# A twelve-layer macaron kernel: the first maxima of the 16-head attentions are computed in the layers before them

## The chip, the cores and the metric

The kernel runs on one core of a Trainium2 chip, as one program. The metric is the device time of one execution in microseconds (us); "before" is the median of three runs. One execution was also profiled, and every view shown comes from it. PE is TensorE (PEld its weight loads), DVE VectorE, ACT ScalarE, POOL GpSimd, SP the queue that issues most DMAs.

## The reference

The input x has 2048 tokens of 128 channels (attentions see it as batches of one sequence; the kernel treats it as 2048 rows). Twelve layers follow each other, each adding to x what it computes from the layer-normed x:

```python
x = x + 0.5 * ffn0(ln(x)); x = x + attn0(ln(x)); x = x + 0.5 * ffn0(ln(x))
x = x + 0.5 * ffn1(ln(x)); x = x + attn1(ln(x)); x = x + 0.5 * ffn1(ln(x))
x = x + 0.5 * ffn2(ln(x)); x = x + attn2(ln(x)); x = x + 0.5 * ffn2(ln(x))
x = x + 0.5 * ffn3(ln(x)); x = x + attn3(ln(x)); x = x + 0.5 * ffn3(ln(x))
```

Four of them matter here.

- `ffn1` is a mixture: a router (a second layer norm, eight logits, softmax, the best two), and for each token a shared and eight routed experts `silu(x Wg) * (x Wu) Wd`, all of them computed for all tokens and weighted with the router's gates.
- `attn1` has 16 heads of 8 channels and no mask: `softmax(q k^T / sqrt(8)) v`, then a projection and a bias.
- `ffn2` quantises the normed x in blocks of 32 channels to a six-bit grid and multiplies by one quantised 128 x 128 weight.
- `attn2` is like `attn1`, with rotary embedding on q and k and no bias.

## The kernel before, in words

The 2048 tokens are four chunks of 512 (`NC` = 4, `CH` = 512), each of four blocks of 128 (`TC` = 4). x stays on the chip as `xs[0..3]`. `STAGES` lists the twelve layers; each is a `Stage` whose body is a Python generator. A stage yields an estimate in us after each small piece of its front; `io.lead(passed)` in the running stage takes that much off the next stage's due time, and lets it emit its next piece once it is due. So a stage's front is written out beside the work of the stage before. `yield True` ends the front, and the stage then runs when its turn comes. `io.ready(c)` says whether the previous stage has finished chunk c, `io.mark(c)` reports it. A compiler turns the written order into a static order per engine; it may move instructions by its own estimates, but not those given to `tc.keep_in_program_order`, which keep their order among each other. `tc.high_priority()` lets instructions go ahead of earlier ones.

**The mixture** (`ffn1`). For each chunk c and each of nine experts: `up` makes twelve products of 128 x 512 (L227 to L229: values are kept as a high and a low part, three products each) into `pg` and `pu`, ACT takes SiLU (`sg`, L715), DVE multiplies (`h`, L717). One expert later `down` makes `pd` (L725), which DVE adds to x with the gate (L735). After the fifth expert the next chunk's own front (norm, transpose, router) is emitted at once. In chunks 2 and 3, `io.lead(4.3)` follows each expert.

**The 16-head attention** (`packed` and `flash`). Heads are taken four at a time; four groups by four query chunks are 16 iterations. Keys of one group and chunk are stacked by DMA into a tile `km`, queries into `qt` (`stack_k`, `stack_q`, L1379), with each head on 32 rows (high, low, high parts beside each other). Stream A is the first pass: a step is two score matmuls of 32 rows by 128 x 512 (L1069) into one of two double PSUM banks and one DVE maximum over both (`mp`, L1087). An iteration has 4 row blocks x 4 key chunks x 2 head pairs = 32 steps. Then `put_max` writes the maxima, and `put` makes the queries of the second pass (`q2`, L1561). Stream B is the second pass: scores once more (L1190), the exponential on ACT (`pt`, L1199), the products with v (`pv`, L1136). `flash` interleaves A and B by columns: all of iteration 0 of A runs first, then `leads` and a skew say how far A stays ahead of B. All matmuls of A and B keep their program order on PE (`pe`).

What `packed` emits ahead of its turn are norms, transposes and keys of chunks 0 to 2 and the queries of chunk 0. The tiles `km` and `qt`, their memsets on POOL (L1494, L1496), the stacking and all steps come after `yield True`. The hook of the first step makes chunk 3's keys.

**The small layer** (`ffn2`, k = 0). Its chunks 0 to 2 are emitted beside the mixture; at chunk 3 it calls `io.lead(9.0)` nine times, which emits fronts of `attn2` there. `quantised` is some eleven DVE and POOL instructions over 128 x 512 (L776 to L793).

PSUM has three single banks (tag `s2`), two double ones (`s1`) and one for `pv`.

Of the kernel before, what the change touches and what calls it, by code (L numbers as in the profile page):

```python
# [64 lines left out]
def tile_macaron(ctx: ExitStack, tc: tile.TileContext, a: dict, out: bass.AP, stages=STAGES):  # L65
# [159 lines left out]
    def product(ps, w, x, start=True, stop=True):  # L225
        (wh, wl), (xh, xl) = w, x
        nc.tensor.matmul(ps, wh, xh, start=start, stop=False)  # L227
        nc.tensor.matmul(ps, wh, xl, start=False, stop=False)  # L228
        nc.tensor.matmul(ps, wl, xh, start=False, stop=stop)  # L229
# [434 lines left out]
    def ffn1(io, k, w, early):  # L664
# [3 lines left out]
        def front(c, pool):  # L668
            n = 1 if pool is early and k else 2
            xf = layer_norm(c)  # L670
            xT = high_low(turned(xf), pool, "xT", n)
            ps = turned(layer_norm(xf))
            x2 = pool.tile([P, CH], F32, name="x2T", tag="raw", bufs=n)
            nc.vector.tensor_scalar(x2, ps, col("ln_scale"), col("ln_bias"), ALU.mult, ALU.add)
            ps = bank()
# [18 lines left out]
            return xT, gate  # L694
# [3 lines left out]
        cur = front(0, early)  # L698
        yield True
        with tc.tile_pool(name="f1", bufs=1) as pool, tc.tile_pool(name="f1w", bufs=1) as pool_w:  # L700
# [6 lines left out]
            def up(e, xT):  # L707
                w = expert(e)[0]
                pg, pu = banks("pg"), banks("pu")
                for m in range(2):  # L710
                    product(pg[:, m * CH : (m + 1) * CH], part(w, m * P), xT)
                for m in range(2):
                    product(pu[:, m * CH : (m + 1) * CH], part(w, I1 + m * P), xT)
# [6 lines left out]
            def down(c, e, h, gate):  # L720
                wd = expert(e)[1]
                pd = bank("pd").rearrange("p (i c) -> p i c", i=TC)
                for i in range(TC):
                    for m in range(2):
                        nc.tensor.matmul(  # L725
                            pd[:, i, :], h[:, m, i * P : (i + 1) * P], wd[:, m, :],
                            start=m == 0, stop=m == 1,
                        )
# [14 lines left out]
            for c in range(NC):  # L743
                xT, gate = cur
                for n, e in enumerate(order):
                    h = up(e, xT)
                    if n + 2 < len(order):
                        expert(order[n + 2])
                    if last is not None:
                        down(*last)  # L750
                    last = c, e, h, gate
                    if n == 4 and c + 1 < NC:
                        cur = front(c + 1, pool)
                    if n == 0 and c:
                        io.mark(c - 1)
                    if c > 1:
                        io.lead(4.3)
# [5 lines left out]
    def quantised(src, pool, tag, bufs=1):  # L763
# [5 lines left out]
        def new(name, m=n):  # L769
            return pool.tile([P, m], F32, name=name, tag=tag + name, bufs=bufs)  # L770
# [25 lines left out]
    def pre_ffn2(k, pool):  # L796
        if k == 0:
            w = fetch(pool, "l2w", 0, C)
            wqT.append(const.tile([P, P], F32, name="wqT"))
            q = quantised(w, pool, "w")  # L800
# [6 lines left out]
    def ffn2(io, k, w, early):  # L807
        bufs = 2 if k == 0 else 1
        half_bias = early.tile([P, C], F32, name="half_bias")
        nc.vector.tensor_scalar_mul(half_bias, row("bias2"), 0.5)  # L810
        for c in range(NC):
            while not io.ready(c):
                yield 0
            if c == NC - 1:
                yield True
                io.upcoming()
                io.lead(9.0)
            xn = layer_norm(c, True)
            q = quantised(xn.rearrange("p i c -> p (i c)"), early, "x", bufs)
            if io.here():  # L820
                for _ in range(8):
# [3 lines left out]
            qT = early.tile([P, CH], F32, name="qT", tag="qT", bufs=bufs)  # L825
# [9 lines left out]
            io.mark(c)  # L835
            if c < NC - 1:
                yield 1.0
                stats_of[c] = statistics_of(xs[c])

# [130 lines left out]
    def flash(io, pool, early, its, nh, causal, scale, s1, s2, pv_mm, put_max, begin, finish, poll=None,  # L970
              on_exp=None, split_at=1, fill=None, leads=None, hook=None, flush=True, order=None):
# [30 lines left out]
        if halved:  # L1002

            halves = {}
            for name in ("ident", "maskq", "maskk"):
                raw = pool.tile([P, 2, P], F32, name="halfraw", tag="halfraw", bufs=2)
# [5 lines left out]
                halves[name] = pool.tile([P, 2, P], BF16, name="half" + name)  # L1012
# [11 lines left out]
        if tiled and causal:  # L1024
            junk = pool.tile([P, CH], F32, name="junk")
            strip = pool.tile([P, CH], F32, name="strip")
# [4 lines left out]
        last_top = {}  # L1031
# [16 lines left out]

        def stream_a():
            for n, (g, qc) in enumerate(its):  # L1050
                begin(n)
                nk = chunks(qc)
                npair = (nk + 1) // 2
                mp = pool.tile([P, TC, nh, NC], F32, name="mp", tag="mp", bufs=3)
                for pi in range(npair):
                    for r in range(TC):
                        before = hook(n, pi, r) if hook is not None else None
                        if pi == r == 0 and before is None:
                            before = last_top.get(n - 1)
                        for kc in range(2 * pi, min(2 * pi + 2, nk)):  # L1060
                            for j0 in range(0, nh, 2):
                                ps = first_pass_bank()
                                last = causal and kc == qc
                                masked = last and not tiled
                                w = (r + 1) * P if last else CH
                                for j in range(2):
                                    o = j * CH
                                    lhsT, rhs = s1(n, j0 + j, r, kc)
                                    pe(nc.tensor.matmul(  # L1069
                                        ps[:, o : o + w], lhsT, rhs[:, :w], start=True, stop=not masked  # L1070
                                    ))
                                    pos[0] += w
                                if masked:
                                    half_masks([ps[:, j * CH + w - P : j * CH + w] for j in range(2)], "maskq")
                                both = ps.rearrange("p (j n) -> p j n", j=2)
# [1218 lines left out]
```

## Time and profile before

| what | us |
|---|---|
| median of three runs (3770.5 to 3781.5) | 3774.64 |
| the profiled execution's own time | 3769.46 |
| its span, first to last instruction | 3767.7 |
| mixture before `attn1`, first to last SiLU | 638.5 to 810.9 |
| first maximum and first exponential of `attn1` | 837.4, 881.8 |
| mixture before `attn2`, first to last SiLU | 1524.0 to 1696.6 |
| first maximum and first exponential of `attn2` | 1741.1, 1788.4 |
| mean granted TensorE clock, share of full speed | 0.943 |

The page cuts the span in 40 slices of 94 us; a digit is a busy share in tenths. A line of groups reads: source line, engine, operation, output <- input, shapes, count | busy us, mean ns | idle time of the engine before it, and what ended it. A window line has for PE, PEld, DVE, ACT and POOL the busy us and the count, then the clock, the share of DMA engines and GB/s. A wait line reads: engine, line <- what it waited for: us in total, times, longest. A timeline line reads: start, duration, engine, line, operation.

### The profile page before, as it was taken

The page shows a single profiled execution, that of the slowest core. Times are in us where ns is not written, and L with a number is a line of the kernel's source. Part 1 is how long each engine was busy: PE and PEld are TensorE (multiplying, and loading weights), DVE is VectorE, ACT ScalarE, POOL GpSimd, SP SyncE. Part 2 cuts the span into 40 slices and gives each one's busy share as a digit, 9 for nine tenths or more (in the row PEclk, how much of TensorE's full clock was granted, in tenths as well). Part 3 has the DMA queues.
Part 4 walks back from the last instruction along what each step waited for, and adds up shares of the span by engine and source line. Part 5 has one row for each costly group of instructions (what it writes and reads, how often), then busy time and mean ns, then how long its engine had stood idle before and what let it go on. Part 6 is the DMA issues. An engine that isn't in the chain of part 4 may idle for free. (4 is left out here: it accounts for less than half of the span.)

```text
span 3767.7 us, 64628 instructions
## 1 busy us (share of the span) xinstructions
PE 3420.8 (91%) x25325; PEld 1846.5 (49%) x25325; DVE 2870.9 (76%) x4793; ACT 2036.2 (54%) x3838; POOL 828.8 (22%) x830
## 2 busy tenths in 40 slices
PE   7679987978999999996999999888999999999989
PEld 5543356863333333783333333366444444444458
DVE  6488555768999998668899999654777877788862
ACT  3246732325888888421788888732333444444442
POOL 1511124110000000112000000142555445533341
PEclk9779988987999999996999999998899999999999
DMA  3311023000000000102000000012443232221010
GB/s 104 83 49 29 9 81 95 4 26 5 12 12 14 8 3 1 35 1 70 10 14 6 16 5 4 15 46 75 140 147 112 97 106 97 89 63 52 24 34 12
DMA packets 124689, 170.18 MB, mean 45 GB/s; under 512 B 25120, under 2 KB 52514, under 8 KB 124384
## 3 DMA queue, kind: packets, MB, share of 16 engines
q1 hardware_dynamic: 121824, 160.80, 13.7%
q0 software_dynamic: 2560, 5.25, 0.9%
q8 instruction: 199, 3.26, 0.3%
q14 instruction: 106, 0.87, 0.1%
HBM read 101.25 MB, written 45.87 MB: 39 GB/s over the span
## 5 line engine op out<-in xcount | busy, mean ns | idle before, releaser
L1087 DVE TENSOR_REDUCE mp<-s 128x2 f32<-128x1024 f32 (+3 forms) x1440 | 1625.7, 1181 | 88.5 <-PE s L1069 68.1
L1199 ACT ACTIVATE pt<-s 128x512 f32<-128x512 f32 (+1 forms) x2368 | 1220.7, 601 | 216.4 <-PE s L1190 141.8
L1190 PE MATMUL s<-q,km 32*128 32x512 f32 (+2 forms) x2368 | 733.6, 491 | 28.6 <-ACT pt L1199 18.7
L1136 PE MATMUL pv<-pt,v 128*32 128x256 f32 (+1 forms) x8568 | 730.9, 413 | 22.9 <-ACT ov L1577 11.2
L1069 PE MATMUL s<-km,qt 32*128 32x512 f32 (+3 forms) x2368 | 620.0, 507 | 61.1 <-DVE mp L1087 37.1
L1190 PEld LDWEIGHTS s<-q,km 32*128 32x128 f32 (+1 forms) x2368 | 324.1, 184 | 531.6 <-issue 341.3
L1179 ACT ACTIVATE pt<-s 128x512 f32<-128x512 f32 (+3 forms) x640 | 306.2, 530 | 355.7 <-PE s L1171 212.8
L143 POOL TENSOR_TENSOR rs<-rs,minus_half 128x4 f32<-128x4 f32 x56 | 57.5, 1026 | 1543.7 <-DVE rs L142 1542.7
L1993 DVE TENSOR_TENSOR sum<-sum,pt 128x512 f32<-128x512 f32 (+3 forms) x328 | 259.4, 805 | 89.9 <-ACT pt L1179 88.3
L1136 PEld LDWEIGHTS pv<-pt,v 128*32 128x32 f32 x8568 | 169.1, 108 | 316.4 <-issue 146.3
L1171 PE MATMUL s<-q,k 64*128 64x512 f32 (+3 forms) x1920 | 300.0, 403 | 14.7 <-ACT pt L1179 10.4
L1136 PE MATMUL pv<-pt,latv 128*64 128x512 f32 (+3 forms) x1280 | 310.4, 564 | 1.3 <-ACT pt L1179 1.3
L1993 POOL TENSOR_TENSOR sum<-sum,pt 128x512 f32<-128x512 f32 (+1 forms) x200 | 265.6, 1328 | 181.5 <-ACT pt L1179 177.0
L1069 PEld LDWEIGHTS s<-km,qt 32*128 32x128 f32 (+1 forms) x2368 | 236.4, 191 | 124.1 <-DVE mp L1087 82.3
L1171 PEld LDWEIGHTS s<-q,k 64*128 64x128 f32 x1920 | 161.8, 188 | 224.8 <-issue 137.3
L715 ACT ACTIVATE sg<-pg 128x1024 f32<-128x1024 f32 x72 | 73.9, 1027 | 174.4 <-PE pg L229 158.8
L1069 PE MATMUL s<-k,q 64*128 64x512 f32 (+3 forms) x640 | 133.7, 433 | 19.0 <-DVE mp L1087 18.6
L1791 DVE TENSOR_TENSOR rot<-rot,tab 128x512 f32<-128x512 f32 x128 | 87.7, 685 | 74.2 <-PE rot L229 38.4
L725 PEld LDWEIGHTS pd<-l1d,h 128*128 128x128 f32 x1152 | 139.3, 192 | 5.6
L725 PE MATMUL pd<-l1d,h 128*128 128x128 f32 x1152 | 140.1, 275 | 0.0
L717 DVE TENSOR_TENSOR h<-pu,sg 128x1024 f32<-128x1024 f32 x72 | 87.9, 1220 | 60.6 <-PE pu L229 55.7
L1171 PE MATMUL s<-q,two 64*128 64x512 f32 (+3 forms) x640 | 128.0, 368 | 0.0
(575 smaller groups left out, 4696.7 us busy)
## 6 DMA issues: line engine op xcount, KB each, us to landing
tab<-in_l3rope SPq DMA_DIRECT2D x66, 256.0 KB
q<-q SPq DMA_DIRECT2D x32, 512.0 KB
k<-k SPq DMA_DIRECT2D x32, 512.0 KB
l0e<-in_l0e SPq DMA_DIRECT2D x32, 256.0 KB
q<-h SPq DMA_DIRECT2D x32, 256.0 KB
q<-rot SPq DMA_DIRECT2D x32, 256.0 KB
k<-h SPq DMA_DIRECT2D x32, 256.0 KB
k<-rot SPq DMA_DIRECT2D x32, 256.0 KB
```

What stands on the lines that cost most here:

```text
L715: nc.scalar.activation(sg, pg, AF.Silu)
L717: nc.vector.tensor_tensor(h.rearrange("p m n -> p (m n)"), pu, sg, ALU.mult)
L725: nc.tensor.matmul(pd[:, i, :], h[:, m, i * P : (i + 1) * P], wd[:, m, :], start=m == 0, stop=m == 1,)
L1069: pe(nc.tensor.matmul(ps[:, o : o + w], lhsT, rhs[:, :w], start=True, stop=not masked))
L1087: ins = nc.vector.tensor_reduce(mp[:, r, j0 : j0 + 2, kc], both[:, :, :w], AX.X, ALU.max,)
L1136: i = pe(nc.tensor.matmul(pv[out_rows, lo:hi], lhsT, pts[j][:, lo:hi], start=kt == 0, stop=kt == nt - 1 and hi == CH))
L1171: pe(nc.tensor.matmul(outs[j][:, c0:], lhsT, rhs[:, c0:], start=i == 0, stop=i == len(terms[0]) - 1 and not diag,))
L1179: ex = nc.scalar.activation(pts[j][:, c0:], outs[j][:, c0:], AF.Exp, scale=scale)
L1190: pe(nc.tensor.matmul(ps[:, c0:], lhsT, rhs[:, c0:], start=i == 0, stop=i == len(terms) - 1 and (tiled or not diag),))
L1199: ex = nc.scalar.activation(pt[:, c0:], ps[:, c0:], AF.Exp, scale=scale)
L1791: nc.vector.tensor_tensor(t.bitcast(F32), ps, halves["tabs"][i], ALU.mult)
L1993: eng.tensor_tensor(t[:, c0:], other[:, c0:], pts[j][:, c0:], ALU.add)
```

## The change

Part of the two 16-head attentions' stream A is emitted ahead of the attention.

- `flash` becomes a generator with `ahead` = 24. The first 24 steps of iteration 0 (key chunks 0 to 2) are emitted by leading, in `one_bank_pairs`: two single banks and two maxima per step instead of a double bank and one. They stand beside the mixture, eight after each chunk's keys.
- The next 24 are those of iteration 1 over key chunks 0 to 2. They are given a due time of 1e9, so that no lead emits them: for `attn1` they follow the mixture, for `attn2` they are emitted by `lead_all` ahead of `ffn2`'s fourth chunk, which has high priority there. Then come key chunk 3 of both iterations and the rest. `leads` adds 24 steps at the start, going evenly to 0 at the last iteration.
- `stack_k`, `stack_q` and the first three `km` and two `qt` tiles with their memsets move into the front, as do the query products of chunks 1 and 2.
- In the mixture, from chunk 1 on, `up` and `down` keep the program order on PE. There are two `io.lead(3.2)` per expert in chunks 1 to 3. Its own front is emitted in four pieces at experts 3 to 6.
- `lead` serves the two stages ahead, so that before `attn2` the mixture leads `ffn2` and behind it `attn2`, whose fronts no longer wait for `ffn2`'s turn.
- For room, `ffn2`'s two stages share one pool with single buffers, and `attn1` and `attn2` fetch their raw q and k weights into a scratch tile.

The diff, cut to these parts (functions that only moved are left out):

```diff
@@ ffn1 @@
         def front(c, pool):
             xf = layer_norm(c)
+            yield
             xT = high_low(turned(xf), pool, "xT", n)
-            ps = turned(layer_norm(xf))
+            x2 = layer_norm(xf)
+            yield
+            ps = turned(x2)
 ...
+            def keep(c):
+                return tc.keep_in_program_order if c else lambda ins: ins
 ...
-                    h = up(e, xT)
+                    h = up(c, e, xT)
                     if n + 2 < len(order):
                         expert(order[n + 2])
+                    if c:
+                        io.lead(3.2)
                     if last is not None:
                         down(*last)
                     last = c, e, h, gate
-                    if n == 4 and c + 1 < NC:
-                        cur = front(c + 1, pool)
+                    if n == 2 and c + 1 < NC:
+                        nxt = front(c + 1, pool)
+                    if 2 <= n < 6 and c + 1 < NC:
+                        cur = next(nxt)
                     if n == 0 and c:
                         io.mark(c - 1)
-                    if c > 1:
-                        io.lead(4.3)
+                    if c:
+                        io.lead(3.2)
@@ ffn2 @@
             if c == NC - 1:
                 yield True
                 io.upcoming()
-                io.lead(9.0)
+                if k == 0:
+                    io.lead_all()
+            urgent.enter_context(tc.high_priority() if c == NC - 1 and k == 0 else nullcontext())
             xn = layer_norm(c, True)
-            q = quantised(xn.rearrange("p i c -> p (i c)"), early, "x", bufs)
-            if io.here():
-                for _ in range(8):
+            q = quantised(xn.rearrange("p i c -> p (i c)"), early, "x")
+            if io.here() and k:
+                for _ in range(9):
                     io.lead(9.0)
@@ flash @@
+        def one_bank_pairs(n, r, kc, j0, mp):
+            for j in range(2):
+                ps = bank()
+                lhsT, rhs = s1(n, j0 + j, r, kc)
+                pe(nc.tensor.matmul(ps, lhsT, rhs, start=True, stop=True))
+                pos[0] += CH
+                nc.vector.tensor_reduce(mp[:, r, j0 + j, kc : kc + 1], ps, AX.X, ALU.max)
 ...
         def stream_a():
+            if ahead:
+                mps = [early.tile([P, TC, nh, NC], F32, name=f"mp{n}") for n in range(2)]
+                for n in range(2):
+                    begin(n)
+                    yield from some(n, [(r, [kc]) for kc in range(NC - 1) for r in range(TC)], mps[n])
+                waiting[0] = False
+                for n in range(2):
+                    yield from some(n, [(r, [NC - 1]) for r in range(TC)], mps[n])
+                    maxima(n, mps[n])
 ...
-        while alive[0] and pos[0] < end[0]:
+        if ahead:
+            waiting[0] = True
+            for i in range(2 * ahead):
+                leading[0] = i < ahead
+                step_a()
+                yield
+        first = end[0] + ahead * 2 * CH
+        while alive[0] and pos[0] < first:
             step_a()
 ...
-            leads = np.diff(starts)
+            leads = np.diff(starts) + ahead * 2 * CH * np.linspace(1, 0, len(its))
@@ packed, ahead of yield True @@
+        if not causal:
+            new_k(early)
+            new_q(early)
         for c in range(1 if causal else NC - 1):
             while not io.ready(c):
                 yield 0
-            front(c)
+            xn = layer_norm(c, False)
+            if not causal:
+                yield 1.5
+            front(c, xn)
             yield 1.5
             queries_or_keys(1, c)
             if c == 0:
                 queries_or_keys(0, c)
             yield 1.5
             if causal:
                 values(c)
+                continue
+            stack_k(0, c)
+            keyed[0] = c + 1
+            if c == 0:
+                stack_q(*its[0])
+            if c < 2:
+                new_k(early)
+            if c == 0:
+                new_q(early)
+            yield 3.0
+            for _ in range(2 * TC):
+                next(flow)
+                yield 1.0
+            if c:
+                queries_or_keys(0, c)
+                if c == 1:
+                    stack_q(*its[1])
+                yield 1.5
+        if not causal:
+            for _ in range(2 * TC * (NC - 1)):
+                yield 1e9
+                next(flow)
         yield True
@@ Stage @@
+        def lead_all(self):
+            s = line[self.n + 1]
+            while not s.led:
+                s.step()
+
         def lead(self, passed):
-            if self.n + 1 < len(line):
-                s = line[self.n + 1]
+            for s in line[self.n + 1 : self.n + 3]:
                 s.due -= passed
                 if s.steps is not None and not s.led and s.due <= 0.0:
                     s.step()
```

## Prediction

> **What bounds the kernel now.** I read the windows first, stage by stage, then the groups and waits of the first 16-head attention, then the timeline at the two seams where a 16-head attention (`attn1`, `attn2`) begins.
>
> Busy time by stage. Columns: PE, weight loads, DVE, ACT, POOL, each with its count, then the granted clock and DMA.
> ```profile
> 900.00:1200.00 300.00, 292.08 (x2946) 113.37 (x2946) 288.89 (x291) 262.38 (x506) 0.00 (x0) 1.00 0.05 12
> 1800.00:2100.00 300.00, 289.37 (x2899) 111.54 (x2895) 287.85 (x288) 258.13 (x499) 2.55 (x2) 1.00 0.05 11
> 674.10:712.40 38.30, 38.30 (x242) 34.07 (x241) 27.72 (x87) 11.59 (x12) 3.31 (x3) 1.00 0.00 1
> 758.10:797.30 39.20, 38.45 (x235) 33.65 (x234) 23.70 (x64) 11.26 (x12) 2.28 (x2) 1.00 0.01 1
> 815.80:837.40 21.60, 5.95 (x22) 4.36 (x22) 10.00 (x22) 5.75 (x12) 7.49 (x13) 0.65 0.19 49
> 837.40:876.00 38.60, 25.78 (x66) 9.46 (x66) 38.49 (x37) 0.00 (x0) 0.00 (x0) 0.50 0.09 24
> 1701.50:1750.20 48.70, 27.17 (x88) 17.28 (x86) 36.80 (x77) 13.64 (x27) 19.57 (x25) 0.66 0.37 110
> ```
> Inside both attentions DVE is busy 96%, ACT 87%. In the mixture (`ffn1`, 674 and 758) PE is full and DVE is not. At the first seam DVE has 10.00 of 21.60 us of work, then 38.6 us of maxima while ACT does nothing. Where PE clock reads 0.50 the maxima still keep DVE full.
>
> Groups and waits of the steady stretch, 900 to 1480 us:
> ```profile
> L1087 DVE TENSOR_REDUCE mp<-s 128x2 f32<-128x1024 f32 x466 | 538.4, 1217 | 8.1 <-PE s L1069 7.2 <-PE s L1190 0.7
> ACT pt L1199 <- PE s L1190: 38.4, 114, 1.2
> PEld s L1069 <- DVE mp L1087: 2.9, 12, 0.4
> ```
> 466 maxima in 580 us is 1.245 us each; DVE idled 8.1 us for them. DVE sets the pace, with ACT and PE not far behind (ACT waits 38.4 us for scores).
>
> Timeline at the seams:
> ```profile
> 814.30 0.86 DVE L735 SCALAR_TENSOR_TENSOR x<-pd,gate,x 128x128 f32<-128x128 f32 x3
> 834.20 0.59 SPq L1379 DMA_DIRECT2D qt<-qL  x1
> 836.54 0.32 PEld L1069 LDWEIGHTS s<-km,qt 32*128 32x128 f32 x4 [6.70 <-issue]
> 837.40 36.29 DVE L1087 TENSOR_REDUCE mp<-s 128x2 f32<-128x1024 f32 x32 [5.97 <-PE s L1069]
> 881.76 2.56 ACT L1199 ACTIVATE pt<-s 128x512 f32<-128x512 f32 x5
> 1742.38 0.40 PE L229 MATMUL rot<-xH,w1L 128*128 128x512 f32 x1
> 1742.71 0.50 PE L1069 MATMUL s<-km,qt 32*128 32x512 f32 x2
> 1743.14 0.94 PE L1338 MATMUL bank<-l2a,vall 128*128 128x128 f32 x6
> 1788.41 2.56 ACT L1199 ACTIVATE pt<-s 128x512 f32<-128x512 f32 x5
> ```
> The mixture's last update of x ends at 817.5; the first exponential is 64.3 us later. For the second attention it is 1702.7 to 1788.4, 85.7 us, with one `ffn2` chunk in it. The 32 maxima of iteration 0 come at 1.13 us each.
>
> **The change part by part.** A "step" below is one pair of score matmuls and its maximum (32 per iteration). Per attention, 24 steps of iteration 0 (three of four key chunks) go into the mixture, 24 of iteration 1 into the seam.
>
> *The attention itself.* DVE has 24 steps less inside the stage: 24 x 1.13 = 27 us. As DVE is at 96% and the order of A and B is respaced evenly, I take 26; bounds 13 (PE, about 1.0 us per cycle at its fastest, or ACT takes over) and 30 (24 x 1.245). Two attentions: -52 us.
>
> *First seam.* Before 64.3 us. After: 24 steps of iteration 1 at 1.13 (27), the fourth chunk's norm, splits and statistics (6), 8 steps of iteration 0 (9), and from the last maximum to the first exponential 8.1 as now (873.7 to 881.8). DVE-bound sum 50, taken 51: -13 us. The fourth chunk's keys are ready sooner than the 24 steps end (here in about 20 us), so they hide it.
>
> *Second seam.* Before 85.7 us. The chunk's own chain (norm, quantise, product, norm, rotated keys, stack) read from its rows at half clock is 36 us; the 24 steps fill its DVE holes and each may hold a chain instruction by up to 1.2 us, in all 8. Then 9 and 8.1: 61, taken 62: -24 us.
>
> *The clock in the seam.* The row 837 to 876 has matmuls in 25.78 of 38.60 us and clock 0.50 all the same. The Trainium skill ("TensorE: Matmul & The Clock Gate", Part 1) says that about 3.4 us of sustained activity release the full clock; by that, 24 more steps in the seam would lift it and take about 3 us off each chain. The trace shows that steps paced by DVE don't, so I take the half clock.
>
> *What the mixture pays on PE.* The row: from the last 128-row matmul (1742.38) over the pair (1742.71) to the next 128-row one (1743.14) is 0.76 us, against 0.23 for two neighbours of one shape, so a step costs 0.53. Its streaming alone would be 0.23, as the two run side by side. The skill ("TensorEngine Tiling (Array Packing)", Key Properties) says that changing the tiling mode drains the TensorE; it speaks against putting 32-row pairs between 128-row products, and here it is paid twice per step. By streaming 24 steps cost 5.5 us, by the row 12.7. I take the row: +12.7 in each mixture. Two query products more in `attn1` (3 x 0.2265 each): +1.4. In the mixture before `attn2` the three fronts that ran in the seam move in: a turn (0.5) and 12 products (2.7) each: +9.7.
>
> *What it pays on DVE.* Leading steps take two single-bank maxima. Between the 366 ns of the 256-wide form and 1217 of the 1024-wide, 512 is an estimated 650, so 1.30 a step. From 674 to 815.8 DVE has 47 us free, plus 14 of the new PE time, against 31 + 1.4: it fits. From 1562 to 1701.5 (100.1 busy of 139.5) it has 39 + 22 against 31 + 3 x 7.3 = 53: nearly full. The mixture's own front, in pieces over experts 3 to 6, meets the 8 steps there: 4 x 2.35 + 9 + 10.4 = 29 of DVE against 24 of PE. One expert of lag is absorbed; I take 2 us each for chunks 1 and 2: +4 per mixture.
>
> *The wait that is added.* From chunk 1 on, products, down products and score pairs keep the written order. A pair whose keys are not stacked stops everything of the mixture behind it on PE, and with it SiLU on ACT and the updates on DVE. In the first mixture the first pair stands four lead calls behind the norm: two experts (9.0) and the front's own products (2) = 11 us. Now a led front takes 7.65 us from statistics (776.63) to the low keys (784.3), after 1.5 for x; three stacking DMAs of 0.6 and 1.75 from issue end to use (834.8 to 836.5) are 3.5: ready at 12.7. Late by 1.7 (chunks 1, 2) and 3.5 (chunk 0, queries too): +7. In the second the first pair stands nine calls behind: 20.3 + 6.3 of other products = 26.6 us; ready at about 17 (`ffn2` chunk, 1645 to 1661.9) + 7.65 + 3 (rotation) + 3.5 + 1 = 32: late by 6 three times: +18. Bounds: 0 (PE runs behind its calls anyhow) to 12 and 15 per chunk (DVE's queue lengthens every link).
>
> *Queues.* SP gets 3 key stacks and 2 query stacks per attention earlier, 15 DMAs; from chunk 1 on no expert weight is still to load, so nothing waits there. POOL gets five of eleven memsets (0.53 each) and, before `attn2`, the rotations' sums (1.26 each) in the mixture, where it is busy under 10%: 0, inside the DVE estimate if they block it. `ffn2`'s single buffers and its shared pool: 0, for its chunks are already one after another; without that cover 2 us a chunk. The other stages keep their order: 0.
>
> **Sum.** Gains 52 + 13 + 24 = 89. Costs 12.7 x 2 + 1.4 + 9.7 = 36.5 and waits 7 + 18 + 4 x 2 = 33: 69.5. Net -19.5 us on the profiled execution's 3769.46: 3750. The median of the runs stands 5 above it: **3755 us**. By place: `attn1` -14, `attn2` -5.5.
>
> **The rivals.**
> 1. *Slower: the fixed order makes PE wait at the first pair of each chunk.* It decides from 89 - 36.5 = 52.5 us of waits, 8.8 per chunk for six. Against it: the led chain of 7.65 us is short. For it: in the second mixture DVE is nearly full, and each link goes through DVE. With 10 us a chunk in the first and 15 in the second, 75 us: net +22, **3797**.
> 2. *Nearly no change: DVE's relief is not cashed,* because exponentials and PE take over at once (ACT 87%, 38.4 us of waits on scores). Half of 52 is lost: +6.5, **3781**. Against it: at the attention's end exponentials alone run at 0.51 us each, 34 us per iteration against 39.
> 3. *The waits vanish,* since PE trails its calls: gains 89 - 36.5 = 52: **3722**.
> 4. *The steps don't fit:* before `attn2` the last of 18 calls per chunk is the eighth step, with none to spare. What is left runs in the seam at 1.13 us each: a few us, within the forecast's own range.
>
> **How the numbers follow.** Forecast 0.48 (own range 3735 to 3772: 0.40 faster, 0.08 same), rival 1 0.27 (0.25 slower), rival 2 0.11 (0.07 same, 0.04 slower), rival 3 0.14 (all faster). A measurement of this kernel can tell about 0.3%, 11 us, from no change. Faster 0.54, same 0.17, slower 0.29. The range goes from rival 3 with the upper bound of the attention's gain (3715) to rival 1 and a little beyond (3805).
>
> **What would show it.** Right: the mixtures longer by about 25 and 44 us with PE still full but for waits at the first `s` pair of a chunk; from last x to first exponential about 51 and 62 us; DVE full through the seams; each attention from first exponential to last maximum 26 us shorter. Wrong: PE holes of 10 us and more in the mixture released by `km` DMAs or by `mp` (rival 1); an unchanged length of the attention with DVE under 93% (rival 2); a mixture longer by only 14 and 22 us (rival 3).

## The result, and the profile after

The changed kernel takes 3888.73 us (median of four runs, 3872.93 to 3899.76) against 3772.57 us for the kernel before on the same chip: ratio 1.0302, 95% interval 1.0261 to 1.0344. Timed once more on another chip it gave 1.0271 (1.0243 to 1.03). The forecast was 3755 us with a range up to 3805: the sign was wrong, and the loss, about 116 us, is far outside. (An execution in the chip's slower state, as one of the five of `odd` and one of the four of `after_again` below, is left out of the medians; chips differ by some 0.5%, so kernels of different chips are compared by their ratios to the kernel before.)

The places, from the timelines of ScalarE and VectorE. A mixture runs from its first SiLU to the end of its last; a seam from there to the first exponential of the attention; an attention from its first exponential to its last.

| us | before | after | difference | predicted |
|---|---|---|---|---|
| mixture before `attn1` | 173.4 | 204.8 | +31 | +25 |
| first seam | 69.9 | 54.9 | -15 | -13 |
| `attn1` | 638.7 | 668.2 | +30 | -26 |
| mixture before `attn2` | 173.6 | 253.4 | +80 | +44 |
| second seam | 90.8 | 69.5 | -21 | -24 |
| `attn2` | 647.5 | 661.1 | +14 | -26 |
| sum | | | +118 | -20 |

The span grew by 121.0 us, so everything else together moved by 3. The seams came out as forecast. Both attentions got longer where they should have got shorter, and the second mixture grew by nearly twice the estimate.

First the windows of the changed kernel (busy us and count of PE, weight loads, DVE, ACT, POOL; clock; DMA): the first attention's steady stretch, the second's, and the two seams.

```profile
900.00:1200.00 300.00, 294.43 (x2755) 114.52 (x2757) 269.89 (x266) 253.96 (x482) 0.00 (x0) 0.97 0.04 9
1860.00:2160.00 300.00, 284.39 (x2487) 113.52 (x2485) 268.47 (x273) 226.35 (x428) 3.15 (x3) 0.92 0.04 12
851.00:895.00 44.00, 29.43 (x81) 12.55 (x81) 42.20 (x50) 5.25 (x11) 5.13 (x8) 0.53 0.11 28
1826.00:1894.00 68.00, 42.70 (x154) 22.22 (x154) 61.02 (x96) 9.10 (x19) 9.91 (x12) 0.61 0.09 25
```

In the first attention DVE fell from 288.89 to 269.89 us of 300, and ACT fell with it: 482 instructions, nearly all of them exponentials, in 300 us instead of 506. PE became busier, 294.43 for 292.08, and yet did fewer matmuls, 2755 for 2946, at a clock of 0.97 for 1.00. An engine that shows more busy time for less work is the sign to follow. (The second line begins in the seam, so its counts do not compare with those of before.) The seams are filled by DVE, 42.20 of 44 and 61.02 of 68 us, at little more than half clock, as expected.

The groups of DVE in the steady stretch, 920 to 1500 us, and the waits of the same stretch:

```profile
L1115 DVE TENSOR_REDUCE mp<-s 128x2 f32<-128x1024 f32 x430 | 511.9, 1222 | 33.4 <-PE s L1245 15.5 <-PE s L1097 15.0
```

```profile
PEld pv L1191 <- ACT pt L1254: 66.1, 193, 1.1
PEld s L1245 <- ACT pt L1254: 56.2, 127, 1.6
ACT pt L1254 <- PE s L1245: 41.1, 124, 1.2
ACT pt L1254 <- PE s L1097: 28.6, 90, 1.8
```

A maximum costs what it did (1222 for 1217 ns), but DVE now idles 33.4 us ahead of the maxima where it idled 8.1. DVE is not what became slow.

The seams in the timeline, from the last update of x (L744) to the first exponential (L1254):

```profile
850.55 0.32 DVE L744 SCALAR_TENSOR_TENSOR x<-pd,gate,x 128x128 f32<-128x128 f32 x1
851.25 1.20 DVE L1115 TENSOR_REDUCE mp<-s 128x2 f32<-128x1024 f32 x1
900.20 1.08 ACT L1254 ACTIVATE pt<-s 128x512 f32<-128x512 f32 x2
1832.70 0.32 DVE L744 SCALAR_TENSOR_TENSOR x<-pd,gate,x 128x128 f32<-128x128 f32 x1
1894.82 2.56 ACT L1254 ACTIVATE pt<-s 128x512 f32<-128x512 f32 x5
```

850.87 to 900.20 is 49.3 us (forecast 51), 1833.02 to 1894.82 is 61.8 us (forecast 62).

### The profile page after: what moved, and what is told of

Read it like the earlier page. It is cut to its first block, busy times and chain, and to the rows that moved or that the text cites. A ratio compares the mean times of both kernels' runs of the same rounds, so it can differ in the third digit from the quotient of the medians.

```text
span 3888.7 us, 64714 instructions
## 1 busy us (share of the span) xinstructions
PE 3523.0 (91%) x25325; PEld 1889.8 (49%) x25325; DVE 2904.1 (75%) x4841; ACT 2051.4 (53%) x3838; POOL 825.6 (21%) x830
## 5 line engine op out<-in xcount | busy, mean ns | idle before, releaser
L1115 DVE TENSOR_REDUCE mp<-s 128x2 f32<-128x1024 f32 (+2 forms) x1392 | 1603.8, 1183 | 140.7 <-PE s L1097 84.5
L1254 ACT ACTIVATE pt<-s 128x512 f32<-128x512 f32 (+1 forms) x2368 | 1236.3, 601 | 240.9 <-PE s L1245 152.3
L1191 PE MATMUL pv<-pt,v 128*32 128x256 f32 (+1 forms) x8568 | 740.2, 418 | 22.1 <-ACT ov L1597 9.4
L1245 PE MATMUL s<-q,km 32*128 32x512 f32 (+2 forms) x2368 | 733.2, 488 | 20.1 <-ACT pt L1254 12.6
L1097 PE MATMUL s<-km,qt 32*128 32x512 f32 (+3 forms) x2272 | 636.4, 484 | 63.7 <-DVE mp L1115 46.4
L1245 PEld LDWEIGHTS s<-q,km 32*128 32x128 f32 (+1 forms) x2368 | 309.7, 187 | 521.9 <-issue 285.2
L1097 PEld LDWEIGHTS s<-km,qt 32*128 32x128 f32 (+1 forms) x2272 | 256.5, 195 | 119.0 <-DVE mp L1115 83.4
L734 PE MATMUL pd<-l1d,h 128*128 128x128 f32 x1152 | 154.1, 291 | 0.6 <-DVE x L744 0.6
L734 PEld LDWEIGHTS pd<-l1d,h 128*128 128x128 f32 x1152 | 148.9, 205 | 10.5 <-issue 5.4
L1097 PE MATMUL s<-k,q 64*128 64x512 f32 (+3 forms) x640 | 132.9, 429 | 19.4 <-DVE mp L1115 18.9
L726 DVE TENSOR_TENSOR h<-pu,sg 128x1024 f32<-128x1024 f32 x72 | 87.6, 1217 | 55.6 <-PE pu L229 51.9
```

Of the source, the lines that this page charges most:

```text
L726: nc.vector.tensor_tensor(h.rearrange("p m n -> p (m n)"), pu, sg, ALU.mult)
L734: keep(c)(nc.tensor.matmul(pd[:, i, :], h[:, m, i * P : (i + 1) * P], wd[:, m, :], start=m == 0, stop=m == 1,))
L1097: pe(nc.tensor.matmul(ps[:, o : o + w], lhsT, rhs[:, :w], start=True, stop=not masked))
L1115: ins = nc.vector.tensor_reduce(mp[:, r, j0 : j0 + 2, kc], both[:, :, :w], AX.X, ALU.max,)
L1191: i = pe(nc.tensor.matmul(pv[out_rows, lo:hi], lhsT, pts[j][:, lo:hi], start=kt == 0, stop=kt == nt - 1 and hi == CH))
L1245: pe(nc.tensor.matmul(ps[:, c0:], lhsT, rhs[:, c0:], start=i == 0, stop=i == len(terms) - 1 and (tiled or not diag),))
```

## Experiments: what made the attentions longer

A cycle of the second pass is two score matmuls, two exponentials and eight products with v; beside its two score matmuls (L1190, after the change L1245) stand the two of one step of the first pass (L1069, L1097). All four have 32 rows, and head j of a group sits on rows 32 j to 32 j + 31, in both passes. The first pass takes heads 0, 1 and then 2, 3; the second takes them in the order 2, 3, 0, 1. So the four matmuls touch four different row groups only when the first pass is ahead by an even number of steps. In the kernel before the lead is 36 steps throughout. The change adds a lead that falls evenly from 24 steps to 0, so it is odd half of the time. (Rows and orders are read from the code.)

**The lead kept even, in the changed kernel** (`even`), and the extra lead kept constant instead of falling (`after_const`, shared with a repeat of the changed kernel, `after_again`):

```diff
 even
             target = np.interp(total[0], starts[:-1], knots)
+            if ahead:
+                target = total[0] + 2048 * np.round((target - total[0]) / 2048)
 after_const
-            leads = np.diff(starts) + ahead * 2 * CH * np.linspace(1, 0, len(its))
+            leads = np.diff(starts) + ahead * 2 * CH
```

> The changed kernel with A's lead over B kept to an even number of steps: where the lead shrinks, it drops by two steps at once instead of by one. Theory 1 (row groups): a step's two score matmuls lie on heads 0,1 or 2,3 in turn, and the second pass beside it on the other two heads; a lead of an odd number of steps puts both on the same row groups, and they run one after the other (pairs of 0.72 us instead of 0.50). Then the even lead brings each attention from 668 and 661 us (first to last exponential) to about 610, and the kernel from 3889 to about 3780. Theory 2 (the relief of DVE is not cashed, because ACT and PE are the bound as soon as DVE has less to do, and the lead itself costs): nothing changes, 3889 within 15 us.

> The changed kernel itself, timed once more beside the kernel before. Theory (the uneven lead costs it some 55 us of the kernel with even steps, in whatever run): ratio 1.030 +- 0.004, clock 0.93 to 0.94, the attentions again 20 to 36 us longer than with an even lead, a quarter of the second-pass pairs held up. Rival (part of that difference was a lower clock of the first run alone): ratio 1.020 to 1.026, the attentions only 10 to 20 us longer than with an even lead.

> The changed kernel with the 24 steps of extra lead kept to the end instead of falling evenly to 0, so that the lead is the same even number of steps throughout. Theory of parity: no held-up pairs, as fast as with the lead rounded to even steps (ratio 1.015, between 1.011 and 1.021), attentions 632 to 648 us. Rival (the falling lead helped by spreading the relief of DVE, and the rounding kept that): the attentions 15 us and more longer than with the rounded lead, ratio 1.025 or above.

**The lead made longer in the kernel before**, by one step (`odd`), two (`skew6`) and three (`skew7`):

```diff
-        skew = 4096 if nh == 4 else 1280
+        skew = (4096 if causal else 5120) if nh == 4 else 1280    # skew6: 6144, skew7: 7168
```

> The kernel before with one number changed: in the two unmasked 16-head attentions A runs 37 steps ahead of B instead of 36, an odd number. Nothing is added or removed. Theory 1: all score pairs of both passes collide on their row groups, a cycle on PE takes 1.23 us instead of 1.01, pairs last 0.72 us; each attention becomes longer by 40 to 80 us, the kernel by 80 to 160 (about 3890). Theory 2: one step more of lead makes no difference, 3773 within 10 us.

> The kernel before with the first pass of the two 16-head attentions two steps further ahead of the second (skew 6144 instead of 4096 columns): 38 steps, an even number again. Theory (whether the two passes' score pairs share 32-row groups hangs on the parity of the lead): nothing changes but the two steps more before the first exponential, which come back at the end: 3755, between 3745 and 3765, attentions 635 to 650 us, pairs at 0.50 us. Rival (any longer lead costs, by buffers held longer or a longer start): twice what one step more cost, +40 to +150 us.

> The kernel before with a lead of 39 steps, an odd number (skew 7168 columns). Theory of parity: as slow as with 37 steps, 3830 +- 15, the attentions 35 to 45 us longer each, s pairs at 0.55 us and more in the undisturbed profile. Rival (length of the lead): slower than with 37 steps by another 40 us and more, 3870 or above.

Measured. The last two columns are counted in the timeline from 950 to 1400 us, over cycles with two score matmuls of each pass, eight products with v and nothing else, from the first score matmul to that of the next cycle. "Held up" means that one score matmul shows under 0.45 us; it began after its partner instead of beside it.

| kernel | lead, steps | median us | ratio to before | `attn1`, `attn2` us | held up | mean cycle us |
|---|---|---|---|---|---|---|
| before | 36 | | 1 | 638.7, 647.5 | 0 of 316 | 1.151 |
| `odd` (cycles at full clock) | 37 | 3830.34 | 1.0200 (1.018 to 1.022) | | 250 of 250 | 1.237 |
| `skew6` | 38 | 3752.23 | 0.9993 (0.9986 to 1.0) | 640.7, 657.2 | 0 of 313 | 1.152 |
| `skew7` | 39 | 3832.01 | 1.0198 (1.0181 to 1.0215) | 675.2, 693.6 | 296 of 296 | 1.241 |
| `after_again` | falling by single steps | 3862.64 | 1.0271 (1.0243 to 1.03) | 664.1, 661.1 | 146 of 290 | 1.210 |
| `even` | falling by two at a time | 3812.62 | 1.0154 (1.0124 to 1.0184) | 632.7, 641.9 | 0 of 301 | 1.147 |
| `after_const` | constant, even | 3803.19 | 1.012 (1.0102 to 1.0138) | 628.7, 640.3 | 0 of 320 | 1.147 |

One step more or three more cost 2% of the kernel; two more cost nothing. So it is the parity, not the length, of the lead. An attention's length in one execution moves by some 10 us with the clock: the second of `skew6` ran at 0.96 and took 657.2 us, that of before at 0.99 took 647.5. In the changed kernel the odd steps cost between 44 us (the ratios of `after_again` and `even`, 0.0117 of 3757 us) and 59 us (3862.64 - 3803.19, on one chip): about half of all that the change lost. In the attentions of the profiled executions it is 35.5 + 19.2 = 54.7 us, `even` against the changed kernel. `even` was expected at 3780 with attentions of 610 us and missed that: the held-up pairs went, but there was no relief behind them.

The timelines show what a held-up pair is. First PE in `skew6` (38 steps), then in `skew7` (39 steps); start, duration, line, shape and how many.

```profile
1051.74 0.50 PE L1190 MATMUL s<-q,km 32*128 32x512 f32 x1
1051.74 0.50 PE L1069 MATMUL s<-km,qt 32*128 32x512 f32 x2
1051.75 0.50 PE L1190 MATMUL s<-q,km 32*128 32x512 f32 x1
1052.18 0.64 PE L1136 MATMUL pv<-pt,v 128*32 128x256 f32 x8
```

```profile
1053.89 0.50 PE L1190 MATMUL s<-q,km 32*128 32x512 f32 x1
1053.90 0.72 PE L1069 MATMUL s<-km,qt 32*128 32x512 f32 x2
1054.24 0.39 PE L1190 MATMUL s<-q,km 32*128 32x512 f32 x1
1054.56 0.64 PE L1136 MATMUL pv<-pt,v 128*32 128x256 f32 x8
```

With 38 steps all four start within 0.01 us and end by 1052.25, and the products with v follow 0.44 us after the first start. With 39 steps the second matmul of each pass starts 0.34 us late, and the products follow after 0.67 us. The changed kernel has both pictures by turns; here is a stretch of its first attention that looks like `skew7`:

```profile
1087.08 0.50 PE L1245 MATMUL s<-q,km 32*128 32x512 f32 x1
1087.09 0.72 PE L1097 MATMUL s<-km,qt 32*128 32x512 f32 x2
1087.42 0.39 PE L1245 MATMUL s<-q,km 32*128 32x512 f32 x1
1087.75 0.64 PE L1191 MATMUL pv<-pt,v 128*32 128x256 f32 x8
```

It also bears on why PE looked busier with less work. The windows of `skew6` and `skew7` in their first attention:

```profile
900.00:1200.00 300.00, 291.65 (x2951) 113.18 (x2947) 291.18 (x296) 265.10 (x510) 0.00 (x0) 1.00 0.05 13
```

```profile
900.00:1200.00 300.00, 296.56 (x2777) 112.44 (x2777) 288.66 (x274) 257.02 (x478) 0.00 (x0) 1.00 0.05 11
```

At the same full clock PE's busy time rises by 5 us while its matmuls fall by 6%: two matmuls one after the other keep PE busy for longer than two side by side.

Held-up pairs are not all of the 54.7 us. Counted at full clock alone, the mean cycle of `after_again` is 1.200 us, 0.049 longer than before, about half of what `skew7` adds (0.090), as half of the pairs should give. The rest came with a lower clock. Here are the fifth and the fifteenth of the 16 groups of 64 exponentials in the first attention, first of the changed kernel, then of `even`:

```profile
1066.30:1110.86 44.56, 43.77 (x365) 15.53 (x362) 37.51 (x35) 35.00 (x66) 0.00 (x0) 0.85 0.02 6
1474.39:1534.90 60.51, 57.80 (x388) 22.87 (x385) 42.37 (x77) 36.44 (x70) 2.01 (x2) 0.69 0.00 1
```

```profile
1045.15:1082.75 37.60, 36.39 (x365) 14.11 (x362) 35.37 (x35) 33.92 (x66) 0.00 (x0) 1.00 0.03 7
1437.33:1484.17 46.84, 43.61 (x392) 17.67 (x390) 40.26 (x72) 36.10 (x71) 2.02 (x2) 0.93 0.00 1
```

These two groups hold 7.0 + 13.7 us of the difference, and the fifth of the second attention (clock 0.88) another 5.8: 26.5 us, nearly half, of which held-up pairs explain only a part. `after_again` shows the low clock in the same three groups (0.88, 0.73, 0.88); `even` and `after_const` do not, so the even lead removes it too. But `skew7`, with every pair held up, has 1.00 and 0.93 there in its first attention, and `even_seam` below, with even steps, 0.76 in the fifteenth. What lowers the clock stays open. Nor was the order of the heads changed at an odd lead, which would test the row groups themselves.

## Experiments: what VectorE's relief is worth

**Maxima over half the columns, in the kernel before** (`half_max`). Left out: the other half of the first-pass scores of the two 16-head attentions, so the softmax is shifted by another number.

```diff
-    mp[:, r, j0 : j0 + 2, kc], both[:, :, :w], AX.X, ALU.max,
+    mp[:, r, j0 : j0 + 2, kc], both[:, :, : w if causal else w // 2], AX.X, ALU.max,
```

> The kernel before, where in the two unmasked 16-head attentions each maximum is taken over 256 of a head's 512 columns: half of the first pass's DVE work is left out (the softmax is then shifted by another number), every matmul stays. It asks what a cycle of the attention costs when DVE is no bound at all. If DVE sets the pace, as predicted (1.245 us per step, PE at 1.0), each attention falls from 639 and 648 us by 60 to 90 us. If ACT, PE and the order they share set it nearly as much, by 30 or less: that would be why 24 steps fewer in the attention gave 6 us and not 26.

Measured: 3723.61 us, ratio 0.9922 (0.9904 to 0.9941). But the attentions are 634.4 and 655.6 us long (638.7 and 647.5 before); it is the seams that shrank, from 69.9 to 57.7 and from 90.8 to 77.9. The window of the steady stretch and the group of the maxima from 880 to 1440:

```profile
900.00:1200.00 300.00, 292.24 (x2951) 112.80 (x2947) 179.48 (x296) 263.51 (x510) 0.00 (x0) 1.00 0.05 13
```

```profile
L1087 DVE TENSOR_REDUCE mp<-s 128x2 f32<-128x512 f32 x454 | 313.4, 692 | 194.0 <-PE s L1069 125.3 <-PE s L1190 67.7
```

DVE went from 288.89 to 179.48 us of 300, and the instructions of ACT from 506 to 510. So DVE at 96% did not set the pace of the attention; it only just kept up. The middle of the first attention, 704 exponentials from the third group of 64 to the thirteenth, shows it without the two ends: before, `even`, `half_max`, and for comparison `skew7`:

```profile
969.35:1396.54 427.19, 415.86 (x4218) 160.09 (x4216) 416.62 (x416) 376.23 (x726) 0.00 (x0) 1.00 0.04 10
966.24:1393.40 427.16, 415.05 (x4180) 159.77 (x4179) 397.75 (x400) 377.30 (x728) 0.00 (x0) 1.00 0.04 10
945.49:1372.80 427.31, 416.47 (x4215) 160.27 (x4219) 255.29 (x415) 375.63 (x727) 0.00 (x0) 1.00 0.04 10
962.50:1418.90 456.40, 449.45 (x4213) 169.74 (x4211) 440.28 (x416) 390.68 (x726) 0.00 (x0) 1.00 0.04 9
```

Sixteen DVE instructions fewer, or maxima of half the width, leave the same 427 us; only held-up pairs lengthen it. PE, busy 97%, and ACT, 88%, set the pace between them; which of their mutual waits is the tightest was not tried. (The second attention of `half_max` is longer than before at a clock of 0.96 for 0.99.)

The attentions of `even` are still 6.0 and 5.6 us shorter than before, those of `after_const` 10.0 and 7.2. The part that both share is no relief. In the first attention it lies in the first group of 64 exponentials; here are those of before, `even` and `it0_free`, the last kernel below, which takes no step of iteration 1 ahead and has the lead of before:

```profile
881.76:929.45 47.69, 44.22 (x389) 19.47 (x389) 37.73 (x41) 36.32 (x70) 0.00 (x0) 0.94 0.04 9
884.99:927.81 42.82, 41.73 (x385) 18.75 (x385) 35.06 (x39) 36.11 (x70) 0.00 (x0) 0.94 0.03 8
857.58:899.27 41.69, 40.60 (x390) 18.03 (x391) 37.07 (x40) 35.33 (x68) 0.00 (x0) 0.94 0.02 6
```

`it0_free` has the short start without the led steps, so these do not explain it; what it shares with `even`, the fronts moved into the mixture, was not tried alone. `after_const` gains another 4.8 us in the fifteenth group (41.7 for 46.5), most of which runs after its first pass has ended; that is relief. What a step is worth when the first pass is gone, the last 64 exponentials of before show:

```profile
1487.06:1520.54 33.48, 32.78 (x208) 10.41 (x209) 5.16 (x27) 32.67 (x66) 2.01 (x2) 0.99 0.00 1
```

That is 33.5 us for 64 exponentials, against 427.19 / 11 = 38.8 with 32 steps beside them: an estimated 0.17 us per step, 4 us for 24 steps, near what `after_const` gains there. The forecast had 26.

## Experiments: the mixtures

**All 48 steps in the seam** (`even_seam`: `even`, with the 24 steps of iteration 0 taken out of the mixture and emitted with those of iteration 1):

```diff
-            for _ in range(2 * TC):
-                next(flow)
-                yield 1.0
 ...
-            for _ in range(2 * TC * (NC - 1)):
+            for _ in range(4 * TC * (NC - 1)):
```

> The changed kernel with the even lead, and all 48 leading steps moved out of the mixture into the seam behind it; norms, keys, queries and stacking stay in the mixture, in the fixed order. It tells what the steps cost the mixtures from what the fronts and the order cost. If the steps are what stretches them (204.8 and 253.4 us against 173.5 and 173.6), the mixtures fall to about 180 and 200, and the seams grow by 27 each at most. If it is the fronts and the waits of the fixed order, the second mixture stays above 230.

Measured: 3820.79 us, ratio 1.0163 (1.0132 to 1.0195), no gain over `even`. The mixtures became 183.6 and 217.0 us (`even`: 202.4 and 242.7), the seams 84.5 and 94.0 (54.9 and 70.2). A step therefore costs 18.8 / 24 = 0.78 us beside the first mixture, 25.7 / 24 = 1.07 beside the second, 29.6 / 24 = 1.23 in the first seam and 23.8 / 24 = 0.99 in the second. Led steps are cheaper than steps in the seam in the first place but not yet in the second, and dearer than the 0.53 us read from one row. The attentions became longer too, 642.5 and 651.2 us (632.7 and 641.9), at clocks of 0.97 and 0.96 (0.99 and 0.98); why the clock fell was not tried. Without the led steps the first mixture is still 10 us longer than before.

**The second mixture.** The waits of the changed kernel in it, 1572 to 1826 us, and the matmul groups (L180 transposes the quantised tile of `ffn2`, L1072 are the led score pairs):

```profile
PE turn L180 <- DVE e L807: 25.3, 3, 8.4
PE bank L1072 <- DMA km<-kH: 4.8, 2, 2.7
PE bank L1072 <- DMA qt<-qL: 2.8, 1, 2.8
```

```profile
L180 PE MATMUL turn<-cst,e 128*128 128x128 f32 x12 | 3.4, 435 | 25.3 <-DVE e L807 25.3
L1072 PE MATMUL bank<-km,qt 32*128 32x512 f32 x46 | 14.2, 541 | 7.6 <-DMA km<-kH 4.8 <-DMA qt<-qL 2.8
```

PE stood still three times, 8.4 us each, and not mainly at the score pairs that the forecast watched (7.6 us in all) but at the transpose of each `ffn2` chunk. `ffn2` yields 9.0 after emitting its quantising and before the transpose. The lead calls of 3.2, two per expert, take 9.0 off in three calls, one and a half experts later; before the change the calls were of 4.3, one per expert, three calls being three experts. In the trace of the first such chunk DVE quantises from 1630.89 (L790) to 1638.49 (the end of L807), and PE had reached the transpose at 1638.5 - 8.4 = 1630.1, before the quantising had begun. PE works in the order it was given, so experts behind the transpose wait with it. The granted clock of this mixture fell as well, to 0.89 (0.93 in `after_again`, with the same waits) from 1.00 before.

**The transpose written later** (`even_later`), then **without the fixed order of the mixture's matmuls** (`even_later_free`), and **with the steps in the seam** (`even_later_seam`, the edit of `even_seam`):

```diff
 even_later: even, and in ffn2
-            yield 9.0
+            yield 9.0 if k else 15.0
 even_later_free: even_later, and in ffn1
-                return tc.keep_in_program_order if c else lambda ins: ins
+                return lambda ins: ins
```

> The changed kernel with the even lead, and the small layer's led chunks wait 15 instead of 9 units of lead time between the quantising and its transposes. In the changed kernel's second mixture PE stood 25.3 us at three transposes of the quantised tile, which come in its order before DVE has made it. If those waits are paid in full, the second mixture shrinks by about 20 us against the even lead alone, less 2 or 3 for the steps that no longer fit; if DVE is the bound there, the wait only moves to the next instruction and it shrinks by under 8.

> The changed kernel with the even lead and the later transposes, and the mixture's own matmuls free to be moved by the compiler (no fixed order in chunks 1 to 3; the leading steps keep theirs). If the fixed order costs the waits, the mixtures shrink from 204.7 and 223.9 us by 5 to 20 each. If the order was what kept the steps from being bunched, they grow.

> The changed kernel with the even lead, the later transposes, and all 48 leading steps in the seam. Without steps the mixtures measure the fronts and the fixed order alone: about 184 and 198 us. If a step beside the mixture costs PE 0.53 us, as predicted, they are 13 us shorter than with the steps; measured so far was 19 (0.78 per step) in the first. The seams grow by 24 to 30 us, so the kernel's time stays within 12 us of 3789.

| kernel | median us | ratio to before | mixtures us | seams us |
|---|---|---|---|---|
| `even` | 3812.62 | 1.0154 (1.0124 to 1.0184) | 202.4, 242.7 | 54.9, 70.2 |
| `even_later` | 3789.49 | 1.0088 (1.0066 to 1.011) | 204.7, 223.9 | 54.9, 72.7 |
| `even_later_free` | 3779.66 | 1.0079 (1.0059 to 1.01) | 202.7, 208.2 | 54.6, 77.5 |
| `even_later_seam` | 3811.06 | 1.0159 (1.0141 to 1.0178) | 183.6, 203.5 | 84.5, 95.0 |

The later transpose takes 18.8 us off the second mixture, and the waits of `even_later` in it (1522 to 1750 us) show where from:

```profile
PE turn L180 <- DVE e L807: 7.6, 3, 4.8
PE bank L1072 <- DMA km<-kH: 3.4, 2, 2.1
```

The fixed order costs 2 us in the first mixture and 15.7 in the second, of which 4.8 come back as a longer second seam; the two ratios overlap. Without it the transposes wait 0.3 us in all, and the clock of the second mixture is back at 1.00 (0.96 in `even_later`). With the steps in the seam the price of a led step is confirmed: 21.1 / 24 = 0.88 us in the first mixture, 20.4 / 24 = 0.85 in the second, against 29.6 / 24 = 1.23 and 22.3 / 24 = 0.93 in the seams. It was expected within 12 us of `even_later` and came out 21.6 us slower: the seams grew by 52 us where the mixtures gave back 41.5, and the first attention became 9.9 us longer at a clock of 0.97 for 0.99.

**What is left of the idea when its costs are removed** (`it0_free`). The fronts and the stacking stay led in the mixture; the 24 steps of iteration 0 run in the seam, on double banks; iteration 1 is not taken ahead; the transpose comes later, no fixed order in the mixture. The lead of the attention is the one of before:

```diff
-                for n in range(2):
+                for n in range(1):
                     begin(n)
 ...
-            for i in range(2 * ahead):
-                leading[0] = i < ahead
+            for i in range(ahead):
 ...
-        first = end[0] + ahead * 2 * CH
+        first = end[0]
 ...
-            leads = np.diff(starts) + ahead * 2 * CH * np.linspace(1, 0, len(its))
+            leads = np.diff(starts)
```

> A version meant to keep what paid and drop what did not: fronts, stacking, rotated keys and queries stay in the mixture, with the later transposes; the 24 steps of iteration 0 run in the seam on double banks; iteration 1 is not led, the lead of A is constant and even as before, and the mixture has no fixed order. Expected: mixtures 176 and 190 us, seams 57 and 70 (before 70 and 91), attentions as before (639, 648). In sum 3735 to 3750 against 3753 before on this chip. If the fronts cost the mixture as much as they save in the seam, 3753 to 3765.

Measured: 3743.11 us (3732.5 to 3752.5), ratio 0.9972 (0.9961 to 0.9983): faster than the kernel before, by about 10 us. For `attn1` the mixture pays 5.2 us (178.6), the seam gives back 15.0 (54.9) and the attention 1.4. For `attn2` the mixture pays 25.1 (198.7) for a seam shorter by 24.9 (65.9), an even trade. The largest idle time of PE in that mixture (groups from 1470 to 1680 us) is one expert's products waiting for DVE:

```profile
L227 PE MATMUL pu<-xTH,wgu3H 128*128 128x512 f32 x8 | 3.9, 491 | 7.2 <-DVE h L726 7.2
```

## Why the prediction was wrong, point by point

- **"The attention itself", -26 each: the step that failed.** Its premise, "DVE sets the pace", was read from a busy share of 96% and 8.1 us of idle time. `half_max` took 109 us of 300 off DVE, and 704 exponentials took 427.31 us for 427.19. In `even` the attentions became 6.0 and 5.6 us shorter, and most of that stands at their start, where `it0_free` has it without led steps. The forecast had this as rival 2 at a chance of 0.11, cashing half; the runs cashed at most a quarter. What it held against this rival was the answer: an iteration of 39 us with the first pass and 34 without makes 24 steps worth about 4 us, not 26. Over both attentions this is 40 us of the miss.
- **A cost that no step of the sum contained.** The sentence "the order of A and B is respaced evenly" passed over what the respacing does to the pairs: a falling lead goes through odd steps. That is 55 us in the attentions, partly held-up pairs and partly a lower clock that the even lead also removes, and it turned a missing gain into a loss. No rival named it. The timeline of before had the sign in it, four score matmuls at one start (1051.71 to 1051.72 us, for one), and the code had the condition, the order (2, 3, 0, 1).
- **Mixture before `attn2`, +44: measured +80, of which about 10 belong to that profiled execution** (243.9 us in the repeat, +70; clock 0.89 and 0.93). The mechanism of rival 1, PE held by something that is not ready, was right, but the place was wrong: 25.3 us at the quantised tile's transpose, for which the sum had no term (its 0 for `ffn2` was for the buffers), and 7.6 us at the first pairs, where it put 18. The sum had no term for a lower clock in this mixture either.
- **Step price on PE, 0.53 us by the row rather than 0.23 by streaming:** the choice was right, the size too low. 24 steps cost 18.8 to 21.1 us in the first mixture and 20.4 to 25.7 in the second, not 12.7, though part of that is DVE's and the waits', booked apart in the sum (7 + 4 in the first mixture). So the first mixture as a whole, +31 for +25, was near. The two maxima of a led step took 2 x 682 ns, not 1.30 us; the 366 ns of that estimate was the shortest of all maxima of before, where the 256-wide form takes 412 ns in the mean.
- **Seams, -13 and -24:** right (-15 and -21). The rule of the Trainium skill ("TensorE: Matmul & The Clock Gate", Part 1) that the forecast set aside, full clock after about 3.4 us of sustained activity, would have lifted the clock; with 24 more steps in them the seams ran at 0.53 and 0.61.
- **The balance.** Predicted -20, found +118, a miss of 138 us: 40 the relief, 55 the odd steps, 36 the second mixture, 6 the first, 1 the seams.

## What to carry to other kernels

An engine at 96% that barely waits may only be keeping up: before a relief is booked at full price, ask what the cycle costs without the relieved instruction at all, which the trace often shows somewhere. Two streams of small matmuls that share PE by row groups have a phase, and any edit to how far one leads the other must keep that phase; look for matmuls that start together in the timeline and ask what would part them. When a producer's distance is written as a number of units, recount it if the change alters how fast the units are used up.

## What the runs showed of the hardware that was not expected

- Four 32-row matmuls of 512 columns, two from each stream, start within 0.01 us when the code puts them on four different row groups. When two of them share one, the second starts 0.34 us later, and PE is busy for longer with fewer matmuls: 296.56 us with 2777 against 291.65 with 2951. The row groups themselves are read from the code, the trace shows only the times.
- A phase of one step is worth 2.0% of this kernel (1.0200 and 1.0198 for 37 and 39 steps, 0.9993 for 38).
- A 32-row pair between 128-row products costs 0.78 to 1.07 us, waits included, and the same step alone in the seam, paced by DVE, 0.93 to 1.23.
- DVE at 416.62 us of 427.19 was not what bound the stretch: with 255.29 us the stretch took 427.31.
